# Weights before inputs, bias products through a sum on VectorE, and four weight sums moved into the first turn, in a two-layer graph attention kernel

## The chip, the cores and the metric

The kernel runs on one core of a Trainium2 chip. The metric is the device time of one execution in microseconds (us); several executions are timed and their median is taken. A profile of one execution was recorded too. The engines are called PE (TensorE, with PEld for its weight loads), DVE (VectorE), ACT (ScalarE), POOL (GpSimd) and SP (SyncE, which here only issues DMAs). Each engine takes its own instructions in order.

## The reference

The input is x of shape 128 x 128 x 512 (128 graphs of 128 nodes) and an adjacency of shape 128 x 128 x 128. Two layers follow, each on the rectified layer norm of x, with its result added to x:

```
h = relu(layernorm(x))
m = h @ map_w.T + map_b                          # 8 heads of 64
q = m @ q_w.T + q_b ;  k = m @ k_w.T + k_b
cos_adj = cosine(m, m) > 0.1                     # per head, masked
p = softmax(masked(q k^T / 8))
A = cos_adj * p
x = x + relu(((A @ (h @ gcn_map_w.T + gcn_map_b)) @ gcn_W.T) / (sum(A) + 1))

h = relu(layernorm(x))
x = x + softmax(masked(h Wq (h Wk)^T / 8)) (h Wv) Wo + bo   # 4 heads of 64
```

Since q and k are linear in m, and m is linear in h, the kernel first multiplies the weights together once: q needs map_w.T @ q_w.T as its weight and map_b @ q_w.T + q_b as its bias, and k likewise. All numbers are fp32.

## The kernel before

The 128 graphs are worked on in 64 blocks of two graphs. A list written out by hand, TURN (line 910), gives for one turn the order of all steps, each with the number of blocks by which it lags: in one turn, block b does its layer 0, block b − 1 and b − 2 the rest of layer 0 and the start of layer 1, and so on. The loop at line 1155 runs through the turns and calls the steps; nothing reorders them, so each engine's order is the order of the calls. The products with weights use a scheme with seven products in place of eight for a two by two split (graph halves by feature halves); hence each weight tile (w_qk, w_ms, w_qk1, w_v1) has seven parts, three of them loaded (plus T1) and the others made by four subtractions, SUMS (line 171), in `sums_of_weights` (line 173).

Ahead of the loop stands a preparation (lines 1071 to 1138), which the change is about:

- Line 1072 loads the first block's input xt and its adjacency at (`Block.load`, line 236), on SP's queue. Lines 1078 to 1080 load map_w into mw and q_w transposed into wT_q, four pieces of 256 KB each. `load_biases` (line 102) issues small loads on ACT's queue: bm_col (map_b as a column), bq_col, bk_col, gb_col, two for bd, two for b_ms, one for b_o. Then k_w into two tiles wT_k of 512 KB.
- Lines 1088 to 1093 take block 0 through its layer norm: statistics on DVE (`stats0`), the reciprocal root on POOL (`rstd`), normalization on ACT (`norm0`), a transpose in squares on DVE (`h0`), and a trip through DRAM that completes the transpose: four writes to d_h (`h0_put`, line 211) and later one read into mv (`h0_get`, line 218). `h0_out` (line 350) then makes hT on ACT, and `halves` (line 360) sums and differences of its quarters on POOL.
- On SP's queue there follow, in this order, the d_h writes, gw (gcn_map_w, twice 512 KB), w_ms (four times 256 KB), the read mv, the second block's xt, then w_o1, w_qk1 and w_v1.
- `through_m` (line 128) multiplies mw with q's weights and then with k's into four PSUM banks each, from which ACT writes w_qk (line 142). Between the two calls block 1 goes through its layer norm, to its own d_h writes.
- `bias_through_m` (line 145) makes four of the bias columns: for one output chunk, four products of a 128 x 128 weight piece with one column of bm_col. For q it is called after each quarter of the k product (pb_q), for k after each of four `gcn` calls (pb_k). `gcn` (line 155) multiplies gcn_W into gcn_map_w and has ACT copy the result into w_ms.
- After gcn's second call hT and halves of block 0 are made and the sums of w_qk run on DVE; at the end DVE makes b_q, b_k and b_qk, the four sums of w_ms (line 1137) and b_d.

In turn 0 the first seven products are of kind "qk" (line 407, step `p`), with evictions `r` (ACT or POOL), `u` and `c` (DVE or ACT); then seven of kind "ms" (line 395). The list `later` (line 1140) holds ten small pieces of DVE work on layer 1's weights; one is done after each `u` and each `c` of kind "ms" from turn 0 on (line 1160).

The DMAs of SP and ACT share eight completion counters in turn: a DMA is issued only when the one eight before it, in the order of the built program, has landed. PSUM has eight banks, also used in turn.

Of the kernel before, what the change touches and what calls it, by code (L numbers as in the profile page):

```python
# [8 lines left out]
F32 = mybir.dt.float32  # L9
U8 = mybir.dt.uint8  # L10
AF = mybir.ActivationFunctionType
ALU = mybir.AluOpType
# [3 lines left out]
P = 128  # L16
# [4 lines left out]
def kernel(  # L21
# [21 lines left out]
    nc = tc.nc  # L43
    B, S, D = x.shape
    KC = D // P
    DK = 64
# [8 lines left out]
    SCALE = 1.0 / 8.0  # L55
# [4 lines left out]
    def mm_bank(name):  # L60
        return ps.tile([P, 512], F32, tag="bank", name=name)
# [9 lines left out]
    w_ms = const.tile([P, 7, 2, D], F32, name="w_ms")  # L71
    w_qk = const.tile([P, 7, 2, D], F32, name="w_qk")
    w_qk1 = const.tile([P, 7, 2, INNER], F32, name="w_qk1")
# [5 lines left out]
    b_q = const.tile([P, KC], F32, name="b_q")  # L79
    b_k = const.tile([P, KC], F32, name="b_k")  # L80
# [4 lines left out]
    B11, B21, B22, T1, T2, T3, T4 = range(7)  # L85
# [11 lines left out]
    bm_col = const.tile([P, KC], F32, name="bm_col")  # L97
    gb_col = const.tile([P, KC], F32, name="gb_col")
    bq_col = const.tile([P, KC], F32, name="bq_col")
    bk_col = const.tile([P, KC], F32, name="bk_col")  # L100

    def load_biases(bd):
        for t, src in ((bm_col, map_b), (bq_col, q_b), (bk_col, k_b), (gb_col, gcn_b)):
            nc.scalar.dma_start(out=t, in_=src.rearrange("(c p) -> p c", p=P))
        nc.vector.memset(bd, 0.0)
        for j in range(2):
            nc.scalar.dma_start(
                out=bd[j * DK : (j + 1) * DK, j * DK : (j + 1) * DK], in_=gcn_WT
            )
        for j in range(2):  # L110
            nc.scalar.dma_start(
                out=b_ms[:, j, :HD], in_=map_b[None, j * HD : (j + 1) * HD].broadcast_to([P, HD])
            )
        nc.scalar.dma_start(out=b_o, in_=bo[None, :].broadcast_to([P, D]))
# [10 lines left out]

    def through_m(nm, mw, wT, half, sc, between=None):
        banks = [mm_bank(f"pw_{nm}_{i}") for i in range(KC)]
        for dc in range(KC):  # L130
            for ic in range(KC):
                nc.tensor.matmul(
                    banks[ic],
                    lhsT=mw(dc)[:, ic * P : (ic + 1) * P],
                    rhs=wT(dc),
                    start=(dc == 0),
                    stop=(dc == KC - 1),
                )
            if between:
                between(dc)  # L140
        for ic in range(KC):
            nc.scalar.mul(w_qk[:, BLOCKS[ic // 2][half], ic % 2], banks[ic], sc)


    def bias_through_m(pb, wT, oc):
        for dc in range(KC):
            nc.tensor.matmul(
                pb[:, oc : oc + 1],
                lhsT=wT(dc)[:, oc * P : (oc + 1) * P],
                rhs=bm_col[:, dc : dc + 1],  # L150
                start=(dc == 0),
                stop=(dc == KC - 1),
            )

    def gcn(gw, gb_wide, bd, ic):
# [15 lines left out]
    SUMS = ((T3, B22, T1), (T1, T1, B11), (T2, B22, T1), (T4, B21, T2))  # L171

    def sums_of_weights(w):
        for o, a, b in SUMS:
            nc.vector.tensor_sub(w[:, o], w[:, a], w[:, b])
# [5 lines left out]
    keep1 = ctx.enter_context(tc.tile_pool(name="keep1", bufs=1))  # L181
# [7 lines left out]
    mss = const.tile([P, 3, G, H0, W], F32, name="ms")  # L189
# [864 lines left out]
    def block(b):  # L1054
        if b not in blocks:
            blocks[b] = Block(b)
        return blocks[b]
# [3 lines left out]
    def ahead(b, name, *rest):  # L1061

        done.add((b, name, *rest))
        getattr(block(b), name)(*rest)


    def pieces(*tiles):
        n = KC // len(tiles)
        return lambda c: tiles[c // n][:, (c % n) * D : (c % n + 1) * D]

    with tc.manual_schedule():
        ahead(0, "load")
        mw = keep1.tile([P, Q, G, 2, PR, SQ], F32, tag="s", name="mw")
        mw = mw.rearrange("p q g r c j -> p (q g r c j)")
        wq = keep1.tile([P, Q, G * H0 * SQ], F32, tag="near_mv", name="wT_q")
        wq = wq.rearrange("p q r -> p (q r)")
        chunk = lambda t: t.rearrange("p (c o) -> p c o", o=D)
        for i in range(KC):
            for t, src in ((mw, map_w), (wq, q_wT)):
                nc.sync.dma_start(out=chunk(t)[:, i], in_=src[i * P : (i + 1) * P])  # L1080
        bd = keep1.tile([P, IC, T], F32, tag="k1", name="bd")[:, 0, :P]
        load_biases(bd)
        wk = []
        for i in range(2):
            t = keep3.tile([P, G, D], F32, tag="x1", name=f"wT_k{i}")
            load_weights(t, k_wT[i * 2 * P : (i + 1) * 2 * P])
            wk.append(t.rearrange("p c o -> p (c o)"))
        for g in range(G):
            ahead(0, "stats0", g)
            ahead(0, "rstd", 0, g)  # L1090
            ahead(0, "norm0", g)
        ahead(0, "h0")
        ahead(0, "h0_put")
        gw = []
        t = keep1.tile([P, G, KC, S], F32, tag="h1T", name="gw0")
        gw.append(t.rearrange("p g c s -> p (g c s)"))
        t = keep1.tile([P, Q, 2, IC, G, SQ], F32, tag="s1", name="gw1")
        gw.append(t.rearrange("p q r c g j -> p (q r c g j)"))
        for i in range(2):
            load_weights(chunk(gw[i]), gcn_w[i * 2 * P : (i + 1) * 2 * P])  # L1100
        load_ms()
        ahead(0, "h0_get")
        ahead(1, "load")
        load_weights(w_o1, wo)
        for i in range(2):
            rows = slice(i * HD, (i + 1) * HD)
            for j in range(2):
                load_weights(w_qk1[:, BLOCKS[i][j]], (wq1, wk1)[j][rows])
                load_weights(w_v1[:, BLOCKS[i][j]], wv[rows, j * P : (j + 1) * P])
        gb_wide = keep1.tile([P, IC, T], F32, tag="q1", name="gb_wide")  # L1110
        gb_wide = gb_wide.rearrange("p a b -> p (a b)").rearrange("p (c o) -> p c o", c=KC)
        nc.vector.tensor_copy(gb_wide, gb_col[:, :, None].broadcast_to([P, KC, P]))
        through_m("q", pieces(mw), pieces(wq), 0, SCALE)
        for g in range(G):
            ahead(1, "stats0", g)
            ahead(1, "rstd", 0, g)
            ahead(1, "norm0", g)
        ahead(1, "h0")
        ahead(1, "h0_put")
        pb = mm_bank("pb_q")  # L1120
        through_m(
            "k", pieces(mw), pieces(*wk), 1, 1.0, lambda oc: bias_through_m(pb, pieces(wq), oc)
        )
        nc.vector.tensor_add(b_q, pb[:, :KC], bq_col)
        nc.vector.tensor_scalar_mul(b_q, b_q, SCALE)
        pb = mm_bank("pb_k")
        for ic in range(KC + 1):
            gcn(pieces(*gw), gb_wide, bd, ic)
            if ic < KC:
                bias_through_m(pb, pieces(*wk), ic)  # L1130
            if ic == 1:
                ahead(0, "h0_out")
                ahead(0, "halves", 0)
                sums_of_weights(w_qk)
        nc.vector.tensor_add(b_k, pb[:, :KC], bk_col)
        nc.vector.tensor_sub(b_qk, b_q, b_k)
        sums_of_weights(w_ms)
        nc.vector.tensor_sub(b_d, b_ms[:, 0], b_ms[:, 1])

        later = [("scale", w_qk1, w) for w in (B11, B21)]  # L1140
        later += [("sub", w, *sum) for w in (w_qk1, w_v1) for sum in SUMS]

        def one_piece():
            op, w, o, *ab = later.pop(0)
            if op == "scale":
                nc.vector.tensor_scalar_mul(w[:, o], w[:, o], SCALE)
            else:
                nc.vector.tensor_sub(w[:, o], w[:, ab[0]], w[:, ab[1]])


        halves = (-1, "halves", 0)
        early = [t for t in TURN if t != halves]
        early.insert(early.index((0, "unit", 0)), halves)

        for turn in range(1 + min(t[0] for t in TURN), NB + 4):
            for back, step, *args in early if turn < 2 else TURN:
                b = turn - back
                if 0 <= b < NB and (b, step, *args) not in done:
                    getattr(block(b), step)(*args)
                    if later and turn >= 0 and step in ("u", "c") and args[0] == "ms":  # L1160
                        one_piece()
            blocks.pop(turn - 4, None)

# [45 lines left out]
```

## Time and profile before

| | before |
|---|---|
| three runs, us | 3037.57, 3034.12, 3035.43 |
| median, us | 3035.43 |
| the profiled execution, us | 3033.84 |
| its span in the trace, us | 3032.0 |
| mean granted TensorE clock | 0.996 of full |

Busy time by stretch of the first 75 us (us; matmul count in brackets):

| stretch | PE | DVE | ACT | POOL | DMA GB/s |
|---|---|---|---|---|---|
| 0 to 20 | 12.40 (24) | 3.46 | 2.80 | 2.86 | 252 |
| 20 to 40 | 20.00 (65) | 2.88 | 5.76 | 2.10 | 290 |
| 40 to 60 | 18.44 (164) | 14.24 | 7.93 | 7.32 | 43 |
| 60 to 75 | 15.00 (60) | 9.05 | 1.11 | 2.50 | 0 |

Landing times of some DMAs in that stretch (issue, time to landing, us): first xt 0.72, 3.9; bm_col 0.72, 4.1; gb_col 2.37, 4.6; wT_q 4.62, 2.9, then 7.40, 5.6; wT_k 11.6, 6.7; d_h 14.2, 5.8; gw 16.3, 6.0; mv 21.2, 6.8; second xt 21.6, 7.7; third xt 37.6, 4.0.

A span is measured from the first to the last record of the trace; the execution's own time is 1.84 us longer. In a timeline a line begins with its start and its duration; times in brackets are the idle time of the engine before it and what ended that. An fp32 product appears as two MATMUL records (passes).

### The profile page before, as it was taken

Reading aid. Unit: us, or ns where it says so; the run is one execution under the profiler, and the core shown is the slowest. Engines: PE = TensorE matmul, PEld = TensorE weight load, DVE = VectorE, ACT = ScalarE, POOL = GpSimd, SP = SyncE. Lnnn points to the kernel's source line nnn. Section 1 sums busy time; section 2 is a strip of 40 time slices with the busy share of each in tenths; the row PEclk is TensorE's granted clock in tenths of the full one; section 3 lists DMA queues with packets and bytes.
Section 4 is the critical chain, followed back from the end, with each engine's and each line's share of the span. In section 5 each row is a group of like instructions: output and inputs, shape, how many; then the busy total and the mean of one; then the engine's idle time right before and its main releaser. Section 6 shows DMA issues by size and latency. Waiting matters only on the chain. (4 is left out here: it accounts for less than half of the span.)

```text
span 3032.0 us, 68538 instructions
## 1 busy us (share of the span) xinstructions
PE 2990.2 (99%) x25328; PEld 2372.9 (78%) x25328; DVE 2410.0 (79%) x4563; ACT 1471.3 (49%) x4637; POOL 1768.7 (58%) x2439
## 2 busy tenths in 40 slices
PE   8999999999999999999999999999999999999996
PEld 5788788787787787787787787787787787787775
DVE  3788888888888888888888888888888888888873
ACT  2454454554554554554554554554554554544542
POOL 1566566566566566566566566566565565565552
PEclk9999999999999999999999999999999999999998
DMA  4356556555556555565565565565465465465441
GB/s 155 109 159 185 175 166 182 171 172 182 166 177 182 160 183 182 156 188 177 156 191 177 156 188 182 152 191 181 149 194 179 149 192 181 149 189 181 147 140 56
DMA packets 304830, 508.39 MB, mean 168 GB/s; under 512 B 49264, under 2 KB 181104, under 8 KB 296560
## 3 DMA queue, kind: packets, MB, share of 16 engines
q1 hardware_dynamic: 301792, 503.44, 54.5%
q8 instruction: 201, 3.29, 0.4%
q10 hardware_dynamic: 2704, 0.57, 0.1%
q14 instruction: 133, 1.09, 0.1%
HBM read 273.72 MB, written 230.16 MB: 166 GB/s over the span
## 5 line engine op out<-in xcount | busy, mean ns | idle before, releaser
L617 ACT ACTIVATE s<-s,mx 128x128 f32<-128x128 f32 x1024 | 396.3, 393 | 74.1 <-DVE mx L603 74.1
L513 POOL TENSOR_TENSOR rn<-rn,mhalf 128x8 f32<-128x8 f32 x128 | 213.1, 1665 | 330.6 <-DVE rn L508 258.5
L407 PEld LDWEIGHTS py_qk<-halves,w_qk 128*128 128x128 f32 x3072 | 370.4, 193 | 41.4 <-issue 31.8
L407 PE MATMUL py_qk<-halves,w_qk 128*128 128x128 f32 x3072 | 389.2, 277 | 10.5 <-DVE k L476 6.7
L407 PEld LDWEIGHTS pz_qk<-halves,w_qk 128*128 128x128 f32 x3072 | 369.0, 192 | 28.7 <-issue 28.7
L407 PE MATMUL pz_qk<-halves,w_qk 128*128 128x128 f32 x3072 | 385.7, 275 | 0.0
L407 PEld LDWEIGHTS px_qk<-hT,w_qk 128*128 128x128 f32 x2048 | 244.0, 192 | 39.9 <-issue 32.4
L365 POOL TENSOR_TENSOR halves<-h1T 128x256 f32<-128x256 f32 x64 | 46.6, 728 | 387.9 <-ACT h1T L319 381.0
L812 ACT ACTIVATE s<-s,mx 128x128 f32<-128x128 f32 x512 | 199.2, 390 | 142.7 <-DVE mx L802 142.7
L407 PE MATMUL px_qk<-hT,w_qk 128*128 128x128 f32 x2048 | 256.8, 279 | 3.5 <-DVE mix L713 3.5
L395 PE MATMUL px_ms<-w_ms,hT 128*128 128x512 f32 x512 | 247.2, 605 | 0.0
L890 PE MATMUL py<-w_o,oT 128*128 128x512 f32 x512 | 240.7, 594 | 1.4 <-ACT oT L883 1.4
L395 PE MATMUL py_ms<-w_ms,halves 128*128 128x512 f32 x512 | 240.7, 592 | 0.0
L395 PE MATMUL pz_ms<-w_ms,halves 128*128 128x512 f32 x512 | 240.6, 592 | 0.0
L319 ACT ACTIVATE hT<-mv 128x1024 f32<-128x1024 f32 x64 | 67.6, 1057 | 318.1 <-PE py_ms L395 318.1
L724 POOL TENSOR_TENSOR x<-x,mix 128x512 f32<-128x512 f32 x128 | 162.6, 1271 | 89.5 <-DVE mix L713 57.3
L456 ACT ACTIVATE r_qk<-px_qk,b_k 128x128 f32<-128x128 f32 x256 | 73.2, 368 | 275.6 <-PE px_qk L407 271.2
L617 ACT ACTIVATION_READ_ACCUMULATOR s<-s,mx 128x1 f32 x1024 | 196.6, 192 | 0.0
L395 PEld LDWEIGHTS pz_ms<-w_ms,halves 128*128 128x128 f32 x512 | 97.3, 190 | 122.5 <-issue 107.6
L832 POOL TENSOR_TENSOR s<-s,z 128x512 f32<-128x512 f32 x126 | 128.5, 1041 | 106.0 <-DVE z L822 106.0
L395 PEld LDWEIGHTS px_ms<-w_ms,hT 128*128 128x128 f32 x512 | 92.0, 189 | 99.5 <-issue 91.8
L641 DVE SCALAR_TENSOR_TENSOR s<-pc,s 128x512 f32<-128x512 f32 x256 | 163.6, 680 | 3.3 <-PE pc L557 3.1
(140 smaller groups left out, 7121.8 us busy)
## 6 DMA issues: line engine op xcount, KB each, us to landing
d_h<-hn SPq DMA_DIRECT2D x504, 128.0 KB, 3.7
mv<-d_h SPq DMA_DIRECT2D x126, 512.0 KB, 4.4
d_near<-s SPq DMA_DIRECT2D x248, 256.0 KB, 3.8
near_mv<-d_near SPq DMA_DIRECT2D x62, 1024.0 KB, 5.4
xt<-in_x SPq DMA_DIRECT2D x64, 512.0 KB, 7.3
x<-in_x SPq DMA_DIRECT2D x64, 512.0 KB, 6.3
out<-x SPq DMA_DIRECT2D x128, 256.0 KB, 2.3
d_attn<-s SPq DMA_DIRECT2D x252, 128.0 KB, 2.4
```

What stands on the lines that cost most here:

```text
L319: nc.scalar.activation(t.rearrange("p g c (a j) -> p (g c) a j", a=Q), self.f.pop((key, "moved")).rearrange("p a r j -> p r a j"), func,)
L365: nc.gpsimd.tensor_tensor(S1, A[1][0], A[1][1], ALU.add)
L395: nc.tensor.matmul(bank[:, : rhs.shape[1]], lhsT=src[:, c, :], rhs=rhs, start=(first and c == 0), stop=(c == 1), skip_group_check=True,)
L407: nc.tensor.matmul(bank[:, oc * P : (oc + 1) * P], lhsT=(w_qk1 if layer else w_qk)[:, w, c, oc * P : (oc + 1) * P], rhs=src[:, c, :], star ...
L456: nc.scalar.activation(r[:, cols], X[:, cols], AF.Identity, bias=b_k[:, oc : oc + 1])
L513: nc.gpsimd.tensor_tensor(rn, rn, mhalf[:, :H0], ALU.pow)
L617: nc.scalar.activation(s[:, :, g, par, c, :], s[:, :, g, par, c, :], AF.Exp, bias=mx[:, i : i + 1], accum_out=z[:, h : h + 1],)
L641: nc.vector.scalar_tensor_tensor(sp, cp, 0.1, sp, ALU.is_gt, ALU.mult,)
L724: nc.gpsimd.tensor_add(x1, x1, self.f["mix", g])
L812: nc.scalar.activation(s[:, :, par, c, g, :], s[:, :, par, c, g, :], AF.Exp, bias=mx[:, par, c, g : g + 1], accum_out=z[:, par, c, g : g + 1],
L832: nc.gpsimd.tensor_tensor(s[:, :, par].rearrange("p q c g j -> p q (c g) j"), s[:, :, par].rearrange("p q c g j -> p q (c g) j"), z[:, par ...
L890: nc.tensor.matmul(py, lhsT=self.f["oT"][:, g, c, :], rhs=w_o1[:, c, :], start=(c == 0), stop=(c == IC - 1),)
```

## The change

Three things are edited. First, the loads of mw and wT_q are issued ahead of block 0's load of xt and at. Second, `bias_through_m` is gone. In its place DVE makes, per partition, the sum over the four chunks of a weight row times its bm_col value (`bias_sum`, one tile each for q and k, one instruction with one tensor and three with two), queued after gb_wide and ahead of block 1's statistics; TensorE then sums over the partitions with four products each against a column of ones (`bias_columns`), both after gcn's first call, and into one bank. b_q and b_k are made after the sums of w_qk. Third, the sums of w_ms no longer run ahead of the loop: they are put at the head of `later`, and a piece of `later` is now done after `u` and `c` of kind "qk" as well as "ms".

```diff
-    def bias_through_m(pb, wT, oc):
-        for dc in range(KC):
+    def bias_sum(tag, wT):
+        acc = keep1.tile([P, D], F32, tag=tag, name=f"bias_{tag}")
+        nc.vector.tensor_scalar(acc, wT(0), bm_col[:, 0:1], None, ALU.mult)
+        for c in range(1, KC):
+            nc.vector.scalar_tensor_tensor(
+                acc, wT(c), bm_col[:, c : c + 1], acc, ALU.mult, ALU.add
+            )
+        return acc
+
+    def bias_columns(pb, acc):
+        for oc in range(KC):
             nc.tensor.matmul(
                 pb[:, oc : oc + 1],
-                lhsT=wT(dc)[:, oc * P : (oc + 1) * P],
-                rhs=bm_col[:, dc : dc + 1],
-                start=(dc == 0),
-                stop=(dc == KC - 1),
+                lhsT=acc[:, oc * P : (oc + 1) * P],
+                rhs=mss[:, 0, 0, 0, DK : DK + 1],
+                start=True,
+                stop=True,
             )
...
-        ahead(0, "load")
...
                 nc.sync.dma_start(out=chunk(t)[:, i], in_=src[i * P : (i + 1) * P])
+        ahead(0, "load")
...
+        sum_q = bias_sum("n2", pieces(wq))
+        sum_k = bias_sum("r2", pieces(*wk))
         through_m("q", pieces(mw), pieces(wq), 0, SCALE)
...
-        through_m(
-            "k", pieces(mw), pieces(*wk), 1, 1.0, lambda oc: bias_through_m(pb, pieces(wq), oc)
-        )
-        nc.vector.tensor_add(b_q, pb[:, :KC], bq_col)
-        nc.vector.tensor_scalar_mul(b_q, b_q, SCALE)
-        pb = mm_bank("pb_k")
+        through_m("k", pieces(mw), pieces(*wk), 1, 1.0)
+        pb = mm_bank("pb")
         for ic in range(KC + 1):
             gcn(pieces(*gw), gb_wide, bd, ic)
-            if ic < KC:
-                bias_through_m(pb, pieces(*wk), ic)
+            if ic == 0:
+                bias_columns(pb[:, :KC], sum_q)
+                bias_columns(pb[:, KC:], sum_k)
             if ic == 1:
                 ahead(0, "h0_out")
                 ahead(0, "halves", 0)
                 sums_of_weights(w_qk)
-        nc.vector.tensor_add(b_k, pb[:, :KC], bk_col)
+        nc.vector.tensor_add(b_q, pb[:, :KC], bq_col)
+        nc.vector.tensor_scalar_mul(b_q, b_q, SCALE)
+        nc.vector.tensor_add(b_k, pb[:, KC : 2 * KC], bk_col)
         nc.vector.tensor_sub(b_qk, b_q, b_k)
-        sums_of_weights(w_ms)
         nc.vector.tensor_sub(b_d, b_ms[:, 0], b_ms[:, 1])
 
-        later = [("scale", w_qk1, w) for w in (B11, B21)]
+        later = [("sub", w_ms, *sum) for sum in SUMS]
+        later += [("scale", w_qk1, w) for w in (B11, B21)]
         later += [("sub", w, *sum) for w in (w_qk1, w_v1) for sum in SUMS]
...
-                    if later and turn >= 0 and step in ("u", "c") and args[0] == "ms":
+                    if later and turn >= 0 and step in ("u", "c") and args[0] in ("qk", "ms"):
                         one_piece()
```

More of the change, by code (lines that the diff above doesn't have):

```diff
@@ L124, in load_ms, with through_m @@
                 )
-    def through_m(nm, mw, wT, half, sc, between=None):
+    def through_m(nm, mw, wT, half, sc):
         banks = [mm_bank(f"pw_{nm}_{i}") for i in range(KC)]
@@ L138, in through_m @@
                 )
-            if between:
-                between(dc)
         for ic in range(KC):
             nc.scalar.mul(w_qk[:, BLOCKS[ic // 2][half], ic % 2], banks[ic], sc)
-    def bias_through_m(pb, wT, oc):
-        for dc in range(KC):
+    def bias_sum(tag, wT):
[8 more added lines that the diff above has]
+        for oc in range(KC):
             nc.tensor.matmul(
                 pb[:, oc : oc + 1],
-                lhsT=wT(dc)[:, oc * P : (oc + 1) * P],
-                rhs=bm_col[:, dc : dc + 1],
-                start=(dc == 0),
-                stop=(dc == KC - 1),
+                lhsT=acc[:, oc * P : (oc + 1) * P],
+                rhs=mss[:, 0, 0, 0, DK : DK + 1],
+                start=True,
+                stop=True,
             )
@@ L1119 @@
         ahead(1, "h0_put")
-        pb = mm_bank("pb_q")
-        through_m(
-            "k", pieces(mw), pieces(*wk), 1, 1.0, lambda oc: bias_through_m(pb, pieces(wq), oc)
-        )
-        nc.vector.tensor_add(b_q, pb[:, :KC], bq_col)
-        nc.vector.tensor_scalar_mul(b_q, b_q, SCALE)
-        pb = mm_bank("pb_k")
+        through_m("k", pieces(mw), pieces(*wk), 1, 1.0)
+        pb = mm_bank("pb")
         for ic in range(KC + 1):
             gcn(pieces(*gw), gb_wide, bd, ic)
-            if ic < KC:
-                bias_through_m(pb, pieces(*wk), ic)
+            if ic == 0:
+                bias_columns(pb[:, :KC], sum_q)
+                bias_columns(pb[:, KC:], sum_k)
             if ic == 1:
```

## The prediction

> **What bounds the kernel now.** I read the page first (busy shares), then the waits of TensorE over the whole run, then the timeline of the first 80 us, the only place the change touches, and last the DMA landings there.
>
> From the page and from the view of TensorE's waits over the whole run (us in total, times, longest):
>
> ```profile
> PE 2990.2 (99%) x25328; PEld 2372.9 (78%) x25328; DVE 2410.0 (79%) x4563; ACT 1471.3 (49%) x4637; POOL 1768.7 (58%) x2439
> ...
> PE pw_q L132 <- DMA wT_q<-in_q_wT: 7.6, 1, 7.6
> PE pt L297 <- POOL s L830: 7.2, 1, 7.2
> PE px_qk L407 <- DVE mix L713: 3.5, 1, 3.5
> PE py_qk L407 <- DVE kT L476: 2.2, 3, 1.6
> ```
>
> TensorE is idle 3032.0 − 2990.2 = 41.8 us in all, 7.6 of them before its first product. So the end is set by TensorE: every us by which it is further ahead when the loop is entered should arrive at the end, provided nothing else becomes late in the first 80 us. The timeline there (start, duration, engine, line):
>
> ```profile
> 0.72 0.43 SPq L245 DMA_DIRECT2D xt<-in_x  x1
> 1.72 0.46 SPq L1080 DMA_DIRECT2D mw<-in_map_w  x1
> 4.62 0.34 SPq L1080 DMA_DIRECT2D wT_q<-in_q_wT  x1
> 4.63 0.69 DVE L195 BATCH_NORM_STATS2 st<-xt 128x6 f32<-128x512 f32 x1 [3.54 <-DMA xt<-in_x]
> ...
> 14.19 1.89 SPq L211 DMA_DIRECT2D d_h<-hn  x4
> ...
> 21.63 0.43 SPq L245 DMA_DIRECT2D xt<-in_x  x1
> ...
> 27.12 0.95 PE L147 MATMUL pb_q<-bm_col,wT_q 128*128 128x1 f32 x8
> ...
> 27.93 3.68 PE L132 MATMUL pw_k<-wT_k,mw 128*128 128x512 f32 x8
> ...
> 29.39 0.69 DVE L195 BATCH_NORM_STATS2 st<-xt 128x6 f32<-128x512 f32 x1 [16.99 <-DMA xt<-in_x]
> ...
> 33.81 1.25 DVE L305 STREAM_TRANSPOSE hn<-hn 128x1024 f32<-128x1024 f32 x1 [2.64 <-ACT hn L285]
> ...
> 40.91 1.14 PE L158 MATMUL pg<-bd,gw 128*128 128x128 f32 x8
> ...
> 42.70 1.14 PE L158 MATMUL pg<-bd,gw 128*128 128x128 f32 x8
> ...
> 49.06 5.71 DVE L175 TENSOR_TENSOR w_ms<-w_ms 128x1024 f32<-128x1024 f32 x4
> ...
> 56.12 2.02 PE L407 MATMUL py_qk<-halves,w_qk 128*128 128x128 f32 x16 [1.56 <-DVE kT L476]
> ```
>
> To see: the first q weights are issued only at 4.62 (the issue waits for xt to land, since the DMAs share eight completion counters in turn); the bias products stand in the middle of TensorE's stream; the second xt lands at 29.4; and the w_ms sums hold up the first kT on DVE, so TensorE stands 1.56 us.
>
> **What the Trainium skill says.** "DMA: Bandwidth & Descriptors", Anatomy of one DMA, gives a fixed cost of about 2 us plus the bytes; here 256 KB of wT_q issued at 4.62 released TensorE at 7.60, 3.0 us, which agrees. The same page, Queues, rings and completion order, says that descriptors of a ring are taken in order: so SP's transfers queue behind each other, as the landings here do (d_h, gw, w_ms, mv, xt in turn). "TensorE: Matmul & The Clock Gate", Part 1, says that matmuls begin at half rate for some 3.4 us of activity: here the weight loads stand 0.86 us apart from 7.60 to 12.03 and 0.43 after it, so an earlier start brings its slow phase along and gains nothing there. "VectorE: DVE Perf Modes", the perf-mode tier table, has fp32 tensor_scalar at 2x and tensor_tensor at 1x; here 0.42 and 0.68 us for 128x512.
>
> **The change part by part.**
>
> *Weights first.* mw and wT_q (256 KB each) now go out at about 0.7 and 1.2, with no counter to wait for. The same 512 KB as one xt, issued at 0.72, released DVE at 4.63; with the second half issued 0.5 later I take 4.7 for TensorE's start. Bounds: 1.2 + 3.0 = 4.2, and, as mw behind xt landed at 6.3 among the small bias loads, 5.5. Gain 7.6 − 4.7 = 2.9. The next pairs: the second wT_q waits for bm_col (0.72 + 4.1 = 4.8), so lands near 8; it is needed 5.5 us after the start, at 10.2. The third waits for gb_col (2.37 + 4.6 = 7.0), lands by 11 to 13, needed near 13.6. Hidden, the third narrowly.
>
> *Bias products on TensorE.* In the k stage groups of eight passes start 27.93 − 23.69 = 4.24 and then 4.33 us apart, where eight at the plain spacing of 0.43 take 3.44: 0.89 for each bias group, four times: 3.56. In the gcn stage the period is 42.70 − 40.91 = 1.79, half of it the bias: again 4 × 0.89 = 3.56. Removed 7.1. Added: eight one-column products, 16 passes against the 64 removed, 16 × 0.111 = 1.8. Net 5.3.
>
> *Bias sums on DVE.* Two tensor_scalar (0.42) and six with two tensors; no row shows the latter from SBUF alone, between 0.42 and the 0.68 of line 641 I take 0.68: 4.9 us in all (3.4 to 4.9). DVE is idle 17 us before the second xt, and the products that read the sums stand near 36 us, so this is hidden; were the cover gone, at most 4.9.
>
> *w_ms sums moved.* 5.7 us leave DVE ahead of the first kT: the 1.56 stall goes. They return as four pieces of about 1.25 to 1.4 behind the kT/qT evictions of turn 0, while products of 1.79 us run; twice a piece is just in time for the next product, which I price at 0.15 (bounds 0 and, if every piece came in front of a late eviction, 4 × 1.4 = 5.6). Their first use, the second w_ms product, comes five us after the third sum. Four w_v sums move from turn 1's second half to the end of turn 0's and its first qk evictions: 0.41 each, nothing to 0.4; I take nothing.
>
> Ceiling for TensorE: 2.9 + 5.3 + 1.56 = 9.8.
>
> *What the first xt is moved past.* It now stands behind eight weight loads on SP; its counter waits for a bd load (near 8), so it is issued near 8.6. Until it lands, 2.0 MB of mw and wT_q, 0.5 of b_ms and b_o and itself must move. In before all of these had landed by 17.0, with the engines nearly empty from 7 to 9 us (43 and 56 GB/s in the table of one-us windows), time which is now used: I take 15 (14 to 16.5). From landing to the end of the transpose the second xt shows 35.06 − 29.39 = 5.7. So the d_h writes, which wait for it at the head of SP, go out at 20.7 rather than 14.2, and gw, w_ms, mv, the second xt and all later weights stand behind them. But in before they were held by a full DMA system; now the backlog is gone by 20. From 20.7 + 1.7 (start of moving): 0.5 + 1 + 1 + 0.5 + 0.5 = 3.5 MB at the 0.36 to 0.40 MB/us of the trace is 9.2 to 9.7: the second xt lands at 32.2 (31 to 34), 2.8 later, though TensorE is 6.5 earlier there.
>
> Behind it in order on ACT: its two normalizations end 4.4 after landing (36.6), then four evictions of pw_k (0.55 each: 38.8), two gcn pairs (1.3), hT (1.07): 41.2, where TensorE would be ready for the first qk product at 49.04 − 2.9 − 5.3 = 40.8. halves takes 2.3 more: 43.5, where the second product would be ready at 42.6. The w_qk sums on DVE (1.25 each, from 38.8) give the third at 42.5, in time; b_k, now behind them, is there at 44.2 and makes r1 0.15 late. Together 0.9 + 0.15 + 0.15 = 1.2.
>
> Sum: 9.8 − 1.2 = **8.6 us**. The profiled execution took 3033.84, its span 3032.0 and 1.84 around it; after, 3025.2 and 3023.4. That execution is 1.6 below the median of 3035.43; carried to the median: **3026.8**.
>
> **The rivals.**
>
> (1) *Nothing is late*: the second xt lands by 31, and the whole 9.8 arrives: 3025.6. For it: there is slack now, DVE waits 17 us for the second xt, and mv, landed at 28.0, is read by hT only at 44.4. Against: 6.5 us of it go to TensorE's lead and the rest to SP's later start.
>
> (2) *SP's delay passes whole to the second xt*: 29.4 + 6.5 = 35.9, 3.7 later than I take, gain 4.9: 3030.5, no measurable change. For it: in before each issue there waited for a landing. Against: those waits came from a full system.
>
> (3) *The w_ms pieces hold the evictions*: 9.8 − 1.2 − 5.6 = 3.0: 3032.4. For it: 1.25 to 1.4 against slots of 1.79 with batch statistics between. Against: the slots hold.
>
> (4) *Slower*: the same chain from the second xt, if SP issues one DMA only at the landing of the one before. Eleven stand ahead of it from the first d_h on; at 2.9 us each (the second set of d_h landed in 2.7 to 3.0 us), and 4.0 for its own landing (as the third xt shows), it lands at 20.7 + 32 + 4 = 56.7, gain 40.8 − 56.7 = −15.9: 3051.3. It decides from a landing at 32.2 + 8.6 = 40.8 on, that is from about half of these waits. For it: SP did wait for other landings before most issues here. Against: with eight counters in turn a DMA waits for the one eight before it, and only mv needs the landing just before.
>
> **How the numbers follow.** Forecast 0.60 (3026.8; own range 3025.8 to 3029.3), (1) 0.16, (2) 0.13, (3) 0.06, (4) with anything unforeseen in the loop 0.05; the loop's own order of instructions is unchanged from the second half of turn 1 on. A change under 0.2% (6.1 us) can't be told from none: faster is forecast and (1), 0.76; same (2) and (3), 0.19; slower 0.05. The range 3024.0 to 3031.5 adds run spread below (1) and takes in (2), and leaves out about 0.15.
>
> **What would show it.** First product at 4.7; the k stage without gaps, 13.7 us long; gcn and bias 6.3 us; d_h at about 20.7, second xt landing near 32.2; first qk product near 41, the first w_ms product near 54.7 against 63.34 now, and this difference unchanged at 150 us and at the end. Wrong if the second xt lands after 35, if a kT or qT eviction shows up in TensorE's waits with over 1 us, or if the lead at 60 us is lost by the end.

## The result, and the profile after

| | before | after |
|---|---|---|
| median of 22 runs, us | 3035.78 | 3031.26 |
| lowest and highest, us | 3033.86, 3037.57 | 3029.64, 3033.90 |
| span of the profiled execution, us | 3032.0 | 3028.3 |
| ratio after to before | | 0.9986 (95% interval 0.9979 to 0.9992) |

The change gains 4.5 us, half of the 8.6 that were forecast. The time lies inside the stated range, next to the 3030.5 of the rival that forecast no measurable change; with 22 runs each the gain is small but clear, since the whole interval lies below 1.

From the page of the kernel after, and from the view of TensorE's waits over its whole run (us in total, times, longest):

```profile
PE 2986.7 (99%) x25280; PEld 2368.8 (78%) x25280; DVE 2415.7 (80%) x4571; ACT 1469.4 (49%) x4637; POOL 1767.9 (58%) x2439
...
PE pw_q L132 <- DMA wT_q<-in_q_wT: 5.1, 1, 5.1
...
PE pg L165 <- ACT w_qk L140: 2.9, 1, 2.9
PE py_qk L414 <- POOL halves L373: 1.8, 2, 1.5
...
PE px_qk L414 <- ACT r_qk L463: 0.9, 1, 0.9
PE px_qk L414 <- ACT hT L326: 0.4, 1, 0.4
PE py_qk L414 <- DVE kT L483: 0.4, 1, 0.4
```

The first wait fell from 7.6 to 5.1 and the stall on kT almost went, as planned. But there are waits which the kernel before did not have: 2.9 for the evictions of pw_k, 0.9 for r_qk, 0.4 for hT, and one of 0.4 more for halves (before, the wait for halves was a single one of 1.5). All of them stand at the end of the preparation and in the first products of turn 0. TensorE's idle time over the whole run is 3028.3 − 2986.7 = 41.6 us, as good as the 41.8 before: the new waits have taken the place of the old ones. The timeline of the kernel after shows why (start, duration, engine, line, and in brackets the idle time before):

```profile
16.52 0.69 DVE L202 BATCH_NORM_STATS2 st<-xt 128x6 f32<-128x512 f32 x1 [15.43 <-DMA xt<-in_x]
...
22.23 1.78 SPq L218 DMA_DIRECT2D d_h<-hn  x4
...
28.91 0.43 SPq L252 DMA_DIRECT2D xt<-in_x  x1
...
34.34 1.05 PE L165 MATMUL pg<-bd,gw 128*128 128x128 f32 x8
...
36.92 0.69 DVE L202 BATCH_NORM_STATS2 st<-xt 128x6 f32<-128x512 f32 x1 [8.89 <-DMA xt<-in_x]
...
39.19 0.81 ACT L292 ACTIVATE hn<-xt,rstd 128x512 f32<-128x512 f32 x1 [16.31 <-POOL rstd L342]
...
41.21 2.04 ACT L140 ACTIVATE w_qk<-pw_k 128x512 f32<-128x512 f32 x4
...
43.28 5.83 DVE L182 TENSOR_TENSOR w_qk<-w_qk 128x1024 f32<-128x1024 f32 x4 [0.70 <-ACT w_qk L140]
...
45.34 2.37 PE L414 MATMUL px_qk<-hT,w_qk 128*128 128x128 f32 x16 [0.42 <-ACT hT L326]
...
51.07 2.05 PE L414 MATMUL px_qk<-hT,w_qk 128*128 128x128 f32 x16 [0.94 <-ACT r_qk L463]
...
60.10 1.88 PE L402 MATMUL px_ms<-w_ms,hT 128*128 128x512 f32 x4
```

The product of the last line in the kernel before:

```profile
63.34 1.88 PE L395 MATMUL px_ms<-w_ms,hT 128*128 128x512 f32 x4
```

To be seen from top to bottom: TensorE has started 2.5 earlier (at 5.12) and is at the gcn products at 34.3 instead of 40.9. The first xt lands at 16.5 instead of 4.6, and the d_h writes, which need it, go out at 22.2 instead of 14.2. The second xt stands behind them in SP's queue and lands at 36.9 instead of 29.4. ACT has the normalizations of that second xt in its queue ahead of the pw_k evictions, so these run from 41.2 on though the products they read ended near 34.5; gcn's fourth call needs one of their banks and waits until 41.84. On DVE the w_qk sums wait for these evictions too (0.7 us, after the transpose of the second xt), and b_k, for which r_qk waits, stands behind the sums. The first w_ms product starts at 60.10, against 63.34 before: a lead of 3.2, which is the span's 3.7 but for 0.5. In this pair of executions the loop gave nothing back.

The windows of the kernel after show the load on the DMA system in that stretch (us of the window, then its length and the busy time of each engine; the last two columns are the share of the DMA engines that was busy and GB/s):

```profile
14.00:19.00 5.00, 5.00 (x13) 2.20 (x12) 1.64 (x4) 1.47 (x2) 1.22 (x4) 1.00 0.73 254
19.00:23.00 4.00, 4.00 (x11) 1.79 (x10) 2.00 (x4) 3.38 (x6) 0.90 (x3) 1.00 0.00 0
23.00:28.00 5.00, 5.00 (x13) 2.19 (x12) 4.82 (x7) 0.00 (x0) 0.00 (x0) 1.00 0.85 213
28.00:37.00 9.00, 9.00 (x41) 5.41 (x39) 0.11 (x2) 0.00 (x0) 0.00 (x0) 1.00 1.06 373
```

And the second and third of these windows in the kernel before:

```profile
19.00:23.00 4.00, 4.00 (x11) 1.85 (x10) 0.00 (x0) 1.19 (x2) 0.00 (x0) 1.00 1.06 393
23.00:28.00 5.00, 5.00 (x19) 2.61 (x18) 0.00 (x0) 1.19 (x2) 0.00 (x0) 1.00 1.07 371
```

Before, the transfers run without a gap, at 396 GB/s from 14 to 19 and at 393 and 371 after that. After, everything that was issued has landed by 19, SP's head waits for the transpose of the first block, and four us go by with nothing moved; then five more at 213 GB/s.

### The profile page after: what moved, and what is told of

It is laid out like the page before. It is cut to its first block, busy times and chain, and to the rows that moved or that the text cites. A ratio compares the mean times of both kernels' runs of the same rounds, so it can differ in the third digit from the quotient of the medians.

```text
span 3028.3 us, 68452 instructions
## 1 busy us (share of the span) xinstructions
PE 2986.7 (99%) x25280; PEld 2368.8 (78%) x25280; DVE 2415.7 (80%) x4571; ACT 1469.4 (49%) x4637; POOL 1767.9 (58%) x2439
```

## The experiments

Theory A is what the trace suggests: the loss is the late second xt and what stands behind it in order on ACT and DVE. The rivals: (B) the new work on DVE, bias sums and w_ms pieces, costs what is missing, and the order of the loads is a plain gain; (C) the bias products gave nothing for another reason; (D) the late gw, mv or w_ms themselves bind. All ratios below are to the kernel before, run on the same chip.

| kernel | median, us | before, us | ratio | second xt read at | first w_ms product at |
|---|---|---|---|---|---|
| before | 3035.78 | | 1 | 29.39 | 63.34 |
| after | 3031.26 | 3035.78 | 0.9986 (0.9979 to 0.9992) | 36.92 | 60.10 |
| e1_xt_first | 3027.73 | 3035.11 | 0.9975 (0.9966 to 0.9985) | 29.22 | 57.10 |
| e2_xt_after_two_pairs | 3025.38 | 3035.11 | 0.9967 (0.9954 to 0.9979) | 28.77 | 54.67 |
| e3_second_xt_before_gw | 3025.46 | 3035.11 | 0.9969 (0.9958 to 0.9980) | 29.11 | 54.03 |
| e4_bias_on_pe | 3030.98 | 3035.11 | 0.9986 (0.9979 to 0.9993) | 36.46 | 59.05 |
| f5_second_norm_late | 3032.03 | 3035.66 | 0.9989 (0.9982 to 0.9995) | 41.16 | 61.00 |
| f6_pairs_bias_on_pe | 3030.70 | 3035.66 | 0.9984 (0.9978 to 0.9991) | 29.78 | 59.45 |
| f7_pairs_wms_back | 3031.73 | 3035.66 | 0.9987 (0.9978 to 0.9995) | 30.17 | 59.51 |
| f8_weights_first_only | 3037.55 | 3035.66 | 1.0005 (0.9997 to 1.0013) | 38.95 | 66.54 |

The last two columns are from the timelines of one execution each; "read at" is the start of DVE's statistics on the second xt, which in f5 run late by intent. From one row to the next these two measures go together: in the nine changed kernels the gain of the median is the lead at the first w_ms product (63.34 less the last column) plus −0.2 to 1.3 us. So what the preparation wins does reach the end. The spans of the single profiled executions show it less well, since their remainder from that product on differs by up to 3.4 us.

### The load order alone undone: e1

```diff
         for i in range(KC):
+            if i == 0:
+                ahead(0, "load")
             for t, src in ((mw, map_w), (wq, q_wT)):
                 nc.sync.dma_start(out=chunk(t)[:, i], in_=src[i * P : (i + 1) * P])
-        ahead(0, "load")
```

> The changed kernel with block 0's xt and at loaded ahead of mw and wT_q again, as before; the bias sums and the moved w_ms sums stay. Theory A (the changed kernel loses at the second xt: it lands at 36.9 instead of 29.4, because the first xt and with it SP's d_h writes are late, and TensorE's first w_ms product comes 23.2 us after that landing): the first product starts at 7.6, the second xt lands near 29.4, nothing waits for it, first w_ms product at 63.34 - 5.34 - 1.56 = 56.4, 6.9 before that of the kernel before: 3028.9 us, 2.4 faster than the changed kernel's 3031.3. Theory B (the bias sums or the w_ms pieces on DVE cost what is missing, the order of the loads is a plain gain of 2.5): 3031.3 + 2.5 = 3033.8.

Measured 3027.73, 7.4 below the kernel before on its chip. TensorE starts at 7.39 again and waits 1.29 more for the second weight pair, and still the whole is faster than the changed kernel by the medians (about 3 us by the ratios; the intervals overlap a little) and 3.0 ahead of it at the first w_ms product. The second xt is read at 29.22 and the end of the preparation has no wait. Rival B asked for 3033.8 and is out.

### The first xt a little earlier: e2

The same edit with `i == 2`: two pairs of weights, then xt and at, then the other two pairs.

> The changed kernel with block 0's xt and at loaded behind the second pair of mw and wT_q, not behind the fourth. Theory A: the first product still starts at 5.1, the first xt lands near 10, d_h goes out near 16, the second xt lands near 30.5, first w_ms product near 54.0: 9.3 before that of the kernel before, 3026.5 to 3027. Theory B: no change, 3031.3.

Measured 3025.38, 9.7 below the kernel before and, by the ratios, 0.19% or 5.8 us below the changed kernel (five runs; the intervals touch at 0.9979). TensorE's waits in the first 150 us of this kernel:

```profile
PE pw_q L132 <- DMA wT_q<-in_q_wT: 5.4, 2, 5.0
PE px_qk L414 <- DVE mix L720: 3.5, 1, 3.5
PE po L699 <- ACT s L680: 1.6, 1, 1.6
```

The four waits of the changed kernel at the end of the preparation are gone, and the two that follow were there before. The first xt is read at 8.76, the d_h writes go out at 14.56, the second xt is read at 28.77. The start is kept, with one further wait of 0.38 for the third weight pair.

### Only the second xt earlier: e3

```diff
         ahead(0, "h0_put")
+        ahead(1, "load")
         gw = []
...
         ahead(0, "h0_get")
-        ahead(1, "load")
         load_weights(w_o1, wo)
```

> The changed kernel with block 1's xt and at loaded right behind block 0's d_h writes, ahead of gw, w_ms and mv; the first xt stays as late as in the changed kernel. Theory A: the second xt is issued near 24 and lands near 29 to 30, the wait of gcn for the pw_k evictions goes, hT is made near 39; first w_ms product near 54 to 55.5, 3027 to 3028.5. If instead the late mv or gw (both 1.4 us later still) bind: 3029 to 3031. Theory B: 3031.3.

Measured 3025.46. This is the sharpest test of the landing: first xt and d_h writes are as late as in the changed kernel (read at 16.30, issued at 22.03), gw, w_ms and mv are issued 0.8 to 0.9 later still, and only the second xt is read at 29.11 instead of 36.92. Nearly the whole loss is gone, hT runs at 39.58, and TensorE's waits in the first 150 us are

```profile
PE pw_q L132 <- DMA wT_q<-in_q_wT: 5.1, 1, 5.1
PE px_qk L414 <- DVE mix L720: 3.5, 1, 3.5
PE po L699 <- ACT s L680: 1.8, 2, 1.6
PE py_qk L414 <- DVE kT L483: 1.5, 1, 1.5
```

The last of these stands at 114.6, in a later turn. That settles A against D for the late gw, mv and w_ms: they are later here than in the changed kernel, and nothing waits for them.

### The bias products back on TensorE, in both load orders: e4 and f6

`bias_through_m` is called again as in the kernel before, with b_q made ahead of the w_qk sums, and `bias_sum` is left away; in e4 with the loads of the changed kernel, in f6 with those of e2.

> The changed kernel with the bias products of the kernel before (64 passes on TensorE between the k and gcn products) and without the sums on DVE; load order and moved w_ms sums stay. Theory A: TensorE is 5.3 later at the gcn end, which the wait for the second xt (first w_ms product at 36.9 + 23.2 = 60.1) covers but for 0 to 1 us: 3031.3 to 3032.3. Theory C (the 5.3 us do arrive, and something else loses them): 3031.3 + 5.3 = 3036.6.

> The version with xt behind the second pair (3025.4), with the bias products back on TensorE and no bias sums on DVE. Theory A: nothing covers TensorE now, so all 5.3 us show: 3030.7, where the same edit cost nothing in the changed kernel's load order. Theory C (the bias products were covered by something else all along): 3025.4 to 3026.5.

Measured: e4 3030.98, nothing lost against the changed kernel (both 0.9986); f6 3030.70 against 3025.38 of e2, by the ratios 0.17% or 5.2 us, with intervals that touch, and 4.8 at the first w_ms product (59.45 against 54.67). So the 5.3 us that DVE takes off TensorE are real within some us where TensorE sets the pace (f6 against e2), and worth nothing where the second xt does (e4 against after). From e4's timeline:

```profile
50.01 2.05 PE L407 MATMUL px_qk<-hT,w_qk 128*128 128x128 f32 x16
```

The bias products fill the time in which the changed kernel waits: the first qk product is 0.8 later than there (46.14 against 45.34), the third 1.1 earlier (50.01 against 51.07).

### The w_ms sums back ahead of the loop: f7

The load order of e2; `sums_of_weights(w_ms)` stands ahead of b_d again and `later` is as in the kernel before.

> The version with xt behind the second pair (3025.4), with the four w_ms sums ahead of the loop again. On DVE b_qk ends at 43.1; with 5.7 of w_ms sums and 0.7 of b_d the first kT comes at 49.5, and the product that waits for it, wanted at 47.5, starts near 50.2: 2.7 lost, 3028.1. If the moved pieces cost as much as they save: 3025.4; at the 1.56 of the kernel before: 3027.

Measured 3031.73 against 3025.38, by the ratios 0.20% or 6.1 us, with intervals that leave some us of play; the first w_ms product is 4.8 later (59.51 against 54.67). More than any of the three expectations. From f7's timeline:

```profile
42.88 6.53 DVE L182 TENSOR_TENSOR w_ms<-w_ms 128x1024 f32<-128x1024 f32 x4
...
50.76 3.56 PE L414 MATMUL py_qk<-halves,w_qk 128*128 128x128 f32 x16 [3.81 <-DVE kT L483]
```

The sums take 6.53, as they run beside POOL's halves, the wait is 3.81, and the product group after it takes 3.56 instead of 1.95: the granted clock is 0.50 from 50.6 to 54.0. 3.8 + 1.6 = 5.4, of which 0.7 is made up for by a TensorE that was that much ahead of e2's until then. In the kernel before the same sums cost 1.56. Their move is worth far more once TensorE is early.

### The weights first, and nothing else: f8

The kernel before with block 0's load moved behind the loop that loads mw and wT_q.

> The kernel before with the load order alone changed (mw and wT_q ahead of xt and at). Theory A: the first product starts at 5.1, but the second xt lands near 36.9; b_q, the w_qk sums, b_k and the w_ms sums stand behind its transpose on DVE, the first kT comes near 55.9 and the product behind it near 56.6, where it starts at 56.1 in the kernel before: no gain, 3035 to 3036. Theory B (the earlier start is a plain gain): 3035.1 - 2.5 = 3032.6.

Measured 3037.55, ratio 1.0005 with 1 inside the interval: no gain, as A has it and B hasn't (a gain of 2.5), and 1.5 above the upper end of my expectation. The windows of f8 (the third value from the right is the granted TensorE clock):

```profile
43.00:47.00 4.00, 3.12 (x15) 3.12 (x15) 3.11 (x5) 4.00 (x10) 0.00 (x0) 0.50 0.36 84
47.00:51.00 4.00, 4.00 (x20) 4.00 (x20) 3.93 (x3) 1.52 (x5) 3.51 (x3) 0.50 0.86 265
51.00:55.00 4.00, 4.00 (x20) 4.00 (x20) 3.90 (x6) 0.65 (x2) 2.46 (x2) 0.50 0.15 60
```

gcn waits 2.72 for the evictions, until 43.88, and then TensorE runs at half rate until near 55.7 although it is busy in almost all of that time. My expectation lacked two things. The second xt is read at 38.95, 2.0 later than I assumed, though it is issued when it is in the changed kernel (28.95 against 28.91); that puts the end of the w_ms sums at 57.1 and the first kT, behind b_d, near 57.6, and the product that reads it near 58.4 (0.8 behind kT, as in the kernel before), where I had 56.6. The slow products make it 59.40, another 1.0. Both parts are my estimates from this one timeline.

### The second block's norm behind everything: f5

```diff
-        for g in range(G):
-            ahead(1, "stats0", g)
...
-        ahead(1, "h0_put")
         through_m("k", pieces(mw), pieces(*wk), 1, 1.0)
...
                 sums_of_weights(w_qk)
+                nc.vector.tensor_add(b_q, pb[:, :KC], bq_col)
...
+                nc.vector.tensor_sub(b_qk, b_q, b_k)
...
+        for g in range(G):
+            ahead(1, "stats0", g)
...
+        ahead(1, "h0_put")
```

> The changed kernel with its loads as they are (second xt landing near 36.9), but block 1's layer norm (statistics, rstd, normalization, transpose, d_h writes) queued behind the pw_k evictions, hT, the w_qk sums and b_k on ACT and DVE. Theory A (what costs is not the late landing itself but what stands behind it in order on ACT and DVE): the 2.9 us wait of gcn for the pw_k evictions goes, the first qk product comes near 41 rather than 45.3; but r1 now stands behind the normalizations on ACT and holds the third qk product for about 3; first w_ms product near 57 to 57.5, 2.5 to 3 before the changed kernel's 60.1: 3028 to 3029. Theory D (the late gw, mv or w_ms themselves bind): hT stays near 44, 3031.

Measured 3032.03, no better than the changed kernel, where A had 3028 to 3029. The first half of the expectation holds: the wait of gcn is gone and the first qk product starts at 40.24, so it is the order on ACT that made gcn wait and no late weight. The second half is where it failed. From f5's timeline:

```profile
47.16 2.05 PE L414 MATMUL px_qk<-hT,w_qk 128*128 128x128 f32 x16 [3.18 <-ACT r_qk L463]
...
53.03 0.69 DVE L202 BATCH_NORM_STATS2 st<-xt 128x6 f32<-128x512 f32 x1 [2.52 <-DMA xt<-in_x]
...
55.77 3.60 PE L414 MATMUL py_qk<-hT,w_qk 128*128 128x128 f32 x16 [2.44 <-DVE kT L483]
```

The 3.2 for r_qk were expected. But the third block's xt stands on SP's queue behind the second block's d_h writes, which now go out at 47.4; it lands at 53.0, DVE waits for it ahead of the second kT, TensorE loses 2.4 more, and the group after that wait runs at half rate. The same chain, one block on.

## Why the prediction came out as it did

- *What bounds the kernel*: right. TensorE sets the end, and a lead at the first w_ms product reaches it (3.2 and 3.7 of span here, and over all the runs as said below the table).
- *Weights first*, gain of 2.9 from a start at 4.7: 5.12 measured, 2.5. Inside its bounds; the first wT_q, issued at 1.16, released TensorE 4.0 later, where it had been 3.0 in the kernel before (4.62 to 7.60). The slow phase, said to gain nothing, became 0.6 shorter (from the first product to the first of pw_k 15.5 against 16.1). The later pairs were in time.
- *Bias products*, net 5.3: right in size (k stage 34.34 − 20.61 = 13.7; f6 against e2 5.2 by the ratios, 4.8 in the timelines), and the DVE sums hidden: they ended at 28.0, products that read them started at 35.2. They took 5.6 (22.43 to 28.04: two of 0.48 and two rows of three in 2.33), outside the 3.4 to 4.9 that I gave.
- *w_ms sums moved*: the 1.56 stall went, and the pieces cost 0.4 at most (all stalls on kT in the run). Right for this kernel; f7 shows that the price of leaving them, with TensorE early, would have been several us and not 1.56.
- *What the first xt is moved past*: the chain was the right one and its links in the right order, but this is the step that failed, in the landing of the second xt: predicted 32.2, measured 36.9, outside the 31 to 34 that I gave. Of the 4.7, 1.5 are from the first xt (16.5, not 15). The other 3.2 are in the stretch from the first d_h write to that landing. I had 11.5 for it, as the DMA system would be empty; it took 14.7 (22.23 to 36.92), against 15.2 in the full system of the kernel before (14.19 to 29.39). Of the 3.7 to be won back there, 0.5 were. The term that was mis-sized is the 3.5 MB at the rate of a system in full flow, 0.36 to 0.40 MB/us: measured were 0.21 in the first five us, when the system started from empty, and 0.37 in the rest. An estimate from the windows: the 1.07 MB of those five us would take 2.9 at 0.37, so 2.1 were lost there; by 36.9 some 4.4 MB had passed, 0.7 of them weights that stand behind xt in the queue (so the load shared the DMA engines with some issued after it), which is 1.9; and moving began 0.8 and not 1.7 after the first issue, 0.9 won. (The sum has a slip too: 3.5 at 0.40 is 8.8, not 9.2, and in the trace's MB of 10^6 bytes it is 3.67. The two nearly cancel.)
- *Behind it on ACT and DVE*: hT was there 8.4 after the landing (I had 9.0), the second qk product 11.2 after it (11.3). But b_k cost 0.9 and not 0.15: the w_qk sums ran beside POOL's halves and took 5.83 instead of 5.0, and b_q and b_k after them 0.75. So from the landing to the first w_ms product it was 23.2, not 22.5.

With the landing 4.72 later and the stretch behind it 0.64 longer the sum is 8.6 − 5.36 = 3.24, the lead in the timeline. That half of the forecast arrived is no credit to the forecast: its ceiling was right, and the loss it allowed for was 1.2 where 6.6 came.

The slow five us can be taken apart further (kernel after, same columns as above):

```profile
23.00:25.50 2.50, 2.50 (x7) 1.12 (x6) 2.43 (x4) 0.00 (x0) 0.00 (x0) 1.00 0.85 210
25.50:26.00 0.50, 0.50 (x2) 0.21 (x2) 0.46 (x2) 0.00 (x0) 0.00 (x0) 1.00 0.51 41
26.00:28.00 2.00, 2.00 (x6) 0.86 (x5) 1.93 (x3) 0.00 (x0) 0.00 (x0) 1.00 0.93 260
```

From 23 to 25.5 all 571 packets are under 2 KB and carry 0.52 MB, which is just what the four d_h writes hold; from 26 on nearly all packets are larger, those of the loads. So the writes moved alone, at 0.21 MB/us, and the loads behind them began only after that. In the kernel before the small packets pass between 17 and 20 among those of other loads, and the total stays at 374 to 395 GB/s. The length of the gap is not what makes the writes slow: in e2 the second block's writes follow half a us in which nothing moved (34.5 to 35), and from 35 to 37.5, again with small packets alone, they run at 0.20 MB/us.

- *Rival (1)*, nothing late: not the changed kernel, but it is what e2 and e3 do: 9.7 below the kernel before (8.7 and 9.3 at the first w_ms product), where the ceiling was worked out as 9.8.
- *Rival (2)*, SP's delay passes whole to the second xt (35.9, 3030.5): this is nearly what happened, at 36.9 and 3031.3, and I gave it 0.13. Its argument against, that the waits came from a full system, did not hold: with the backlog gone, SP still took 6.7 us from the first d_h write to the issue of the second xt (22.23 to 28.91), against 7.4 before (14.19 to 21.63), and the load then took 8.0 to land, against 7.7.
- *Rivals (3) and (4)*: the pieces held no eviction, and SP did not go landing by landing.

What stays open: why the d_h writes are slow when they run alone (their small packets or their direction would both do; no run separates these), and why the loads behind them need until 28 to come to full flow. e3, with xt instead of gw behind the writes, shows the same: 231 GB/s from 23 to 28. The landing also varies from run to run: f8 has SP's queue of the changed kernel and its second xt came 2.0 later. And b_k's 0.9 is read from the timeline and was not tried by itself.

## What to carry to other kernels

When a load is moved back, follow it through every queue to the last thing that stands behind it: here nothing waited for the load's own data though it came twelve us later (e3), but a write that depends on it sits at the head of SP's queue, and the next block's input behind that. Price such a chain from the moment its head can go, and look for what it will move through an empty DMA system: here the writes alone went at 0.21 MB/us, where the sum had the 0.36 to 0.40 of full flow. And an engine's saved time is worth nothing until the next limit is moved too: the bias products bought nothing in the changed kernel (e4) and some 5 us with the first input a few loads earlier (e2 against f6), and the earlier start lost 3 us (e1) before it won 2.4 (e2 against e1, first w_ms product at 54.67 and 57.10).

## What the runs showed that I had not expected

- A wait of a few us on TensorE can cost more than its length. After the 3.81 of f7 a group of 16 passes took 3.56 instead of 1.95, after the 2.44 of f5 3.60, with the granted clock at 0.50 for 3.4 us each time; in f8, after 2.72, it stayed at 0.50 until near 55.7, with TensorE busy from 43.88 on. It need not: after f5's wait of 3.18 the clock stayed at 1.00. The Trainium skill, "TensorE: Matmul & The Clock Gate", Part 1, gives some 3.4 us of activity for the return to full rate; f7 and f5 agree, f8's record is longer than that. What decided it is not shown.
- The same four w_qk sums took 5.00 us in e2, where they ran ahead of most of the halves on POOL, and 5.83 in the changed kernel, beside them; the second of POOL's halves instructions took 0.73 in e2 and 1.59 in the changed kernel.
